# Two of four batches get their residual added by channels on GpSimd during the recurrence, and the run-up is 10 tokens

## The chip, the cores and the metric

The kernel runs on one core of a Trainium2 chip. Five engines work side by side, each through its own instructions in order: TensorE (PE, with its weight loads shown as PEld), VectorE (DVE), ScalarE (ACT), GpSimd (POOL) and SyncE (SP, which here issues nearly all DMAs). The metric is the device time of one execution in microseconds (us), the median of a few runs. Lower is better.

## The reference

The input is x with 4 batches, 128 channels and 64 x 64 = 4096 tokens, in float32. All arithmetic here is in float32.

```python
x = x + conv_attention(x)                 # layer 0: full softmax attention, 64 wide, 4096 x 4096
t = tokens(x)                             # (4, 4096, 128)
t = t + causal_attention(layernorm(t))    # layer 1: 128 wide
Wx = layernorm(t) @ W.T                   # then normalised over all 4 x 4096 tokens
y0 = 0
y[n] = sigmoid(Wx[n] + y[n-1] @ V.T)      # a recurrence over the 4096 tokens of each batch
t = t + y                                 # the residual; the result goes back to (4, 128, 64, 64)
```

V is orthogonal (128 x 128), and the slope of a sigmoid is at most 0.25, so the state forgets its start quickly.

## The kernel before

There are two paths. `fast_path` does everything and at its end sets a flag when one of its assumptions did not hold; only then `general_path` computes everything again, the recurrence token by token. In the profiled execution only the fast path ran.

**Layers 0 and 1** go batch by batch, and in each by 8 blocks of 512 query tokens. An item is a pair of key tiles: `scores` (L824) writes two 512-wide products into one of two PSUM buffers, ScalarE takes the exponential into `p`, `values` (L885) multiplies it with the values two items later, and VectorE adds `p` up in `dsum` (L875) for the softmax's denominator. Work beside this (finishing a block, projections for the next batch) is cut into small tasks. A task has a slot, counted in items, in which it is due; one task at most is issued in each slot (L988 to L1016). The chain for a block of layer 1 is `finish1` (L721): denominators, projection and residual (`first`), store of the result t to DRAM in the tensor `x2` by tokens (L740), layer norm (`norm`), change from tokens to channels (`second`: VectorE's transpose of 32 x 32 squares at L659 and two rounds of DMAs through DRAM), and `third`: the product with W (L769), its statistics on VectorE (L772), and the store of Wx over the block's own place in `xs` by ScalarE (L782). A scheduler then orders each engine's instructions, so that a task's instructions may stand a little before or after those of its neighbours.

**The recurrence** runs on 256 chunks of 16 tokens at once in each batch, so that a step is one 128 x 256 matmul per batch (L1077), one VectorE instruction (L1079: scale times Wx plus the product) and one ScalarE sigmoid (L1082), for four batches in turn. The start of a chunk is not known, so 11 tokens (`WARM`) of the chunk before are run first from a state of 0.5; after the 16 real steps the end of every chunk is compared with the start that the next chunk used (`gap`, L1106 to L1112), and the norm of the difference per channel over a batch's chunks must be at most `TOL` = 1e-6.

**The residual** (`residual`, L1089) of every batch comes after that. The states lie by channels, the result is stored by tokens: TensorE transposes four 128 x 128 pieces into a PSUM bank (L1096), VectorE adds them into `xr` (L1098), which holds the batch's t as loaded from `x2` (L1033), and after every second addition SyncE issues a store of 512 KB (L1100). There are 32 additions and 16 stores. The host transposes the output at the end.

Of the kernel before, what the change touches and what calls it, by code (L numbers as in the profile page):

```python
# [9 lines left out]
F32 = mybir.dt.float32  # L10
AF = mybir.ActivationFunctionType
ALU = mybir.AluOpType
# [5 lines left out]
CHUNK = 1024  # L18
LN_EPS = 1e-5
BN_EPS = 1e-5  # L20


@with_exitstack
def general_path(
# [11 lines left out]
    f_vT: bass.AP,  # L36
    f_gamma: bass.AP,
    f_beta: bass.AP,
    out: bass.AP,
):  # L40
    nc = tc.nc
    B, C, N = x.shape
# [240 lines left out]
    with tc.tile_pool(name="wx", bufs=1) as wxp, tc.tile_pool(name="fwork", bufs=3) as wk:  # L283
        wx = wxp.tile([P, N, B], F32, name="wx")
        stats = wxp.tile([P, B * NB, nc.vector.BN_STATS_DIM], F32, name="stats")
        with tc.tile_pool(name="ps_ln", bufs=2, space=PSUM) as ps_ln, tc.tile_pool(
            name="ps_wx", bufs=3, space=PSUM
        ) as ps_wx:
            for b in range(B):

                def project(blk, xhat, b=b):
                    wp = ps_wx.tile([P, BLK], F32, tag="w", name="wx_ps")
                    nc.tensor.matmul(wp, lhsT=wf, rhs=xhat, start=True, stop=True)
                    nc.vector.bn_stats(stats[:, b * NB + blk, :], wp)
# [12 lines left out]
        shift = wxp.tile([P, 1], F32, name="shift")  # L307
        nc.vector.tensor_tensor(shift, mv[:, 0:1], scale, ALU.mult)
        nc.vector.tensor_tensor(shift, beta, shift, ALU.subtract)

        STEPS = BLK // B
        with tc.tile_pool(name="ys", bufs=3) as ysp, tc.tile_pool(
            name="ps_y", bufs=2, space=PSUM
        ) as ps_y, tc.tile_pool(name="ps_o", bufs=2, space=PSUM) as ps_o:

            def preload(kb):
                wn = wk.tile([P, STEPS, B], F32, tag="wn", name="wn")
                nc.vector.tensor_scalar(wn, wx[:, ts(kb, STEPS), :], scale, shift, ALU.mult, ALU.add)
                ps = ps_y.tile([P, STEPS, B], F32, tag="y", name="y_ps")
                nc.tensor.matmul(ps, lhsT=ident, rhs=wn, start=True, stop=False, skip_group_check=True)  # L320
                return ps

            nblk = N // STEPS
            prev = None
            nxt = preload(0)
            for kb in range(nblk):
                ps = nxt
                y = ysp.tile([P, STEPS, B], F32, tag="y", name="y")
                for t in range(STEPS):
                    if prev is not None:  # L330
                        nc.tensor.matmul(
                            ps[:, t, :], lhsT=vf, rhs=prev, start=False, stop=t == STEPS - 1, skip_group_check=True
                        )
                    nc.scalar.activation(y[:, t, :], ps[:, t, :], AF.Sigmoid)
                    prev = y[:, t, :]
                    if t == STEPS // 2 and kb + 1 < nblk:
                        nxt = preload(kb + 1)
                o = ysp.tile([P, B, STEPS], F32, tag="o", name="o")
                nc.gpsimd.tensor_tensor(o, xs[:, :, ts(kb, STEPS)], y.rearrange("p t b -> p b t"), ALU.add)
                op = ps_o.tile([P, B, P], F32, tag="o", name="oT_ps")  # L340
                for b in range(B):
                    nc.tensor.transpose(op[:, b, :], o[:, b, :], ident)
                oT = ysp.tile([P, B, P], F32, tag="oT", name="oT")
                nc.vector.tensor_copy(oT, op)
                nc.sync.dma_start(out=out[:, ts(kb, STEPS), :].rearrange("b n c -> n b c"), in_=oT)

# [3 lines left out]
def fast_path(  # L350
# [12 lines left out]
    f_vT: bass.AP,  # L363
    f_gamma: bass.AP,
    f_beta: bass.AP,
    out: bass.AP,
    flag: bass.AP,
):

# [8 lines left out]
    TPB = BLK // P  # L378
    SHIFT = 32.0
    LOW, HIGH = 1e-25, 1e25  # L380
    WARM, TOL, STEPS = 11, 1e-6, 16
    NCH = N // STEPS
    CPB = BLK // STEPS
    S = nc.vector.STREAM_SQUARE_SIZE
# [8 lines left out]

    xs = xpool.tile([P, B, N], F32, name="xs")

    x2 = dram.tile([B, N, P], F32, name="x2")

    def load(engine, name, shape, *parts):
        t = const.tile(shape, F32, name=name)
# [70 lines left out]
    with tc.tile_pool(name="batch", bufs=1) as batch, tc.tile_pool(name="rows", bufs=2) as rowp, tc.tile_pool(  # L470
# [250 lines left out]
        def finish1(b, g):  # L721
# [10 lines left out]
            def first():  # L732
                if final:

                    nc.scalar.activation(spare, agg[:, 0:1], AF.Sigmoid)
                denominators(1, b, g, mem["own"])
                joined(1, b, g, projected(1, agg))
                if final:
                    warm(9, agg[:, : BLK // 2])
                nc.sync.dma_start(  # L740
                    out=x2[b, ts(g, BLK)].rearrange("(j p) c -> p j c", p=P),
                    in_=xs[:, b, ts(g, BLK)].rearrange("p (j c) -> p j c", c=P),
                )
                mem["xh"] = wk.tile([P, TPB, P], F32, tag="xh2", name="xh2")
                mem["of"] = moments(b, g)

# [3 lines left out]
            def second():  # L750
# [9 lines left out]
                for q in range(Q):  # L760
# [2 lines left out]
                        in_=sq[ts(q, S)].rearrange("r c j t -> r c (j t)"),  # L763
                    )
                nc.sync.dma_start(out=mem["xhT"], in_=by_c.rearrange("c r q k -> (c r) (q k)"))

            def third():
                wp = misc("wx_ps")
# [28 lines left out]
            if not final:  # L797
                yield 1, norm
            yield 2, second
            yield 1 if final else 6 if g < 2 or g == NB - 1 else 4, third  # L800


# [219 lines left out]


    with tc.tile_pool(name="xr", bufs=1) as xrp, tc.tile_pool(name="y", bufs=2) as yp, tc.tile_pool(
        name="ps_y", bufs=1, space=PSUM
    ) as ps_y, tc.tile_pool(name="ps_r", bufs=4, space=PSUM) as ps_r:

        HALVES = NCH // P
        by_chunk = lambda t: t.rearrange("b (h q s) c -> b h q s c", q=P, s=STEPS)
        xr = xrp.tile([P, B, HALVES, STEPS, P], F32, name="xr")  # L1030
        for b in range(B):
            for h in range(HALVES):
                nc.sync.dma_start(out=xr[:, b, h], in_=by_chunk(x2)[b, h])  # L1033

        mv = xrp.tile([P, nc.vector.BN_AGGR_DIM], F32, name="mv")
        nc.vector.bn_aggr(mv, ends)
# [17 lines left out]

        assert HALVES * TPB == NB
        early = xrp.tile([P, B, TPB, NCH], F32, name="early")
        late = xs.rearrange("p b (r h k q) -> p b k r h q", h=HALVES, r=TPB, q=P)

        def states(b, s):
            return pair(early[:, b, s]) if s < TPB else late[:, b, s // TPB - 1, s % TPB]

        def step(b, s):

            wx = by_step[:, b, s % STEPS]
            if s == -1:
                y = start[:, b, 1:]
            elif s < 0:
                y = yp.tile([P, NCH], F32, tag=f"y{b}", name="y")  # L1070
            else:
                y = states(b, s)
            if prev[b] is None:
                nc.scalar.activation(grid(y), wx, AF.Sigmoid, scale=scale, bias=shift_half)
            else:
                ps = ps_y.tile([P, NCH], F32, tag=f"y{b}", name="y_ps")
                nc.tensor.matmul(ps if s < 1 else pair(ps), lhsT=vf, rhs=prev[b], start=True, stop=True)  # L1077
                z = yp.tile([P, NCH], F32, tag=f"z{b}", name="z")
                nc.vector.scalar_tensor_tensor(  # L1079
                    grid(z), in0=wx, scalar=scale, in1=grid(ps), op0=ALU.mult, op1=ALU.add  # L1080
                )
                nc.scalar.activation(y, z if s < 0 else pair(z), AF.Sigmoid, bias=shift)  # L1082
            prev[b] = start[:, b, :NCH] if s == -1 else y

        for s in range(-WARM, STEPS):
            for b in range(B):
                step(b, s)

        def residual(b):  # L1089

            for h in range(HALVES):
                for s0 in range(0, STEPS, TPB):
                    part = slice(s0 - TPB, s0 + TPB)
                    ps = ps_r.tile([P, TPB, P], F32, tag="r", name="yT_ps")
                    for j in range(TPB):
                        nc.tensor.transpose(ps[:, j], states(b, s0 + j)[:, h], ident)  # L1096
                    t = xr[:, b, h, ds(s0, TPB)]
                    nc.vector.tensor_tensor(t, t, ps, ALU.add)  # L1098
                    if s0 % (2 * TPB):
                        nc.sync.dma_start(out=by_chunk(out)[b, h, :, part], in_=xr[:, b, h, part])  # L1100

        for b in range(B - 1):
            residual(b)


        gap = xrp.tile([P, B], F32, name="gap")  # L1106
        for b in range(B):
            ps = ps_y.tile([P, NCH], F32, tag=f"y{b}", name="gap_ps")
            nc.tensor.matmul(pair(ps), lhsT=ident, rhs=prev[b], start=True, stop=False)
# [72 lines left out]
```

## Time and profile before

| | us |
|---|---|
| median of 3 runs | 2064.52 (2064.33 to 2066.47) |
| the profiled execution: its time | 2065.22 |
| its span in the profile | 2063.5 |
| last attention instruction (end of the layers) | about 1971 |
| recurrence: first sigmoid to last VectorE step | 1987.21 to 2036.6 |
| 32 residual additions on VectorE | 2036.5 to 2055.9 |
| 16 output stores issued | 2037.8 to 2055.95 |
| span's end | 2063.5 |

The page lists the busy time of each engine, the chain of work that ended last, and the costliest groups. Where times of single instructions are given, they are counted from the start of the span. A line of the windows view gives, for one stretch, the busy time of each engine with its number of instructions, the clock that TensorE was granted (1.00 is full), the mean busy share of the 16 DMA engines and what they moved.

### The profile page before, as it was taken

The page shows a single profiled execution, that of the slowest core. Times are in us where ns is not written, and L with a number is a line of the kernel's source. Part 1 is how long each engine was busy: PE and PEld are TensorE (multiplying, and loading weights), DVE is VectorE, ACT ScalarE, POOL GpSimd, SP SyncE. Part 2 cuts the span into 40 slices and gives each one's busy share as a digit, 9 for nine tenths or more (in the row PEclk, how much of TensorE's full clock was granted, in tenths as well). Part 3 has the DMA queues.
Part 4 walks back from the last instruction along what each step waited for, and adds up shares of the span by engine and source line. Part 5 has one row for each costly group of instructions (what it writes and reads, how often), then busy time and mean ns, then how long its engine had stood idle before and what let it go on. Part 6 is the DMA issues. An engine that isn't in the chain of part 4 may idle for free.

```text
span 2063.5 us, 30798 instructions
## 1 busy us (share of the span) xinstructions
PE 2046.0 (99%) x11716; PEld 896.4 (43%) x11716; DVE 1492.2 (72%) x2865; ACT 990.1 (48%) x1071; POOL 135.5 (7%) x221
## 2 busy tenths in 40 slices
PE   9999999999999999999999999999999999999998
PEld 3333354444333345444333335544433334544456
DVE  4899867455889986644679987754588998764578
ACT  5666633323666643333466663332366664333365
POOL 1000011000000001000000001100000001100000
PEclk9999999999999999999999999999999999999999
DMA  4111012220100111231011101222000111110044
GB/s 113 43 23 23 12 42 51 69 67 16 57 8 17 23 28 46 62 77 41 17 43 22 23 12 42 47 67 72 16 17 5 19 23 28 41 43 25 16 169 165
DMA packets 207148, 89.03 MB, mean 43 GB/s; under 512 B 140960, under 2 KB 189600, under 8 KB 205968
## 3 DMA queue, kind: packets, MB, share of 16 engines
q1 hardware_dynamic: 205984, 86.42, 16.4%
q8 instruction: 94, 1.54, 0.3%
q14 instruction: 62, 0.51, 0.1%
q0 software_dynamic: 288, 0.39, 0.1%
q10 hardware_dynamic: 720, 0.16, 0.0%
HBM read 45.84 MB, written 36.89 MB: 40 GB/s over the span
## 4 chain that ended last, share of the span: by engine, by line
PE 97%; DVE 1%; issue 1%; DMA 0%; ACT 0%; POOL 0%; DVEq 0%; POOLq 0%; ACTq 0%
PE s_ps L844 22%; PE acc L903 22%; PE s_ps L835 22%; PE acc L895 21%; PE o_ps L614 3%; PE y_ps L1077 2%; PE r_ps L577 1%; PE wx_ps L769 1%; PE kr_ps L520 1%; PE v_ps L532 1%; DVE xr L1098 1%; PE warm_ps L484 0%; DMA swap<-kr 0%; ACT p L849 0%; DMA out_x<-xr 0%
## 5 line engine op out<-in xcount | busy, mean ns | idle before, releaser
L875 DVE TENSOR_TENSOR dsum<-dsum,p 128x1024 f32<-128x1024 f32 x676 | 826.0, 1222 | 430.2 <-ACT p L851 312.3
L849 ACT ACTIVATE p<-s_ps,nshift 128x1024 f32<-128x1024 f32 x512 | 569.6, 1117 | 315.0 <-PE s_ps L835 304.4
L851 ACT ACTIVATE p<-s_ps 128x1024 f32<-128x1024 f32 (+2 forms) x288 | 274.5, 953 | 605.5 <-PE s_ps L844 603.2
L895 PE MATMUL acc<-p,v 64*64 64x512 f32 x4096 | 529.2, 590 | 0.0
L835 PE MATMUL s_ps<-swap,kr 64*64 64x512 f32 x2048 | 524.1, 591 | 2.5 <-ACT p L849 1.6
L835 PE MATMUL s_ps<-kr 64*64 64x512 f32 x2048 | 524.1, 591 | 0.0
L844 PE MATMUL s_ps<-rows,xhT 128*128 128x512 f32 (+3 forms) x1152 | 502.9, 559 | 0.0
L903 PE MATMUL acc<-p,xh 128*128 128x512 f32 (+3 forms) x1152 | 500.8, 557 | 0.0
L903 PEld LDWEIGHTS acc<-p,xh 128*128 128x128 f32 x1152 | 216.2, 190 | 244.3 <-issue 233.5
L844 PEld LDWEIGHTS s_ps<-rows,xhT 128*128 128x128 f32 x1152 | 213.8, 190 | 242.4 <-issue 204.6
L895 PEld LDWEIGHTS acc<-p,v 64*64 64x64 f32 x4096 | 155.5, 133 | 281.7 <-issue 269.8
L835 PEld LDWEIGHTS s_ps<-swap,kr 64*64 64x64 f32 x2048 | 139.6, 133 | 141.1 <-issue 125.2
L835 PEld LDWEIGHTS s_ps<-kr 64*64 64x64 f32 x2048 | 139.7, 133 | 138.0 <-issue 133.8
L638 POOL TENSOR_TENSOR ln_rstd<-ln_var,mhalf 128x4 f32<-128x4 f32 x64 | 89.4, 1397 | 1102.1 <-DVE ln_var L636 1102.1
L883 DVE TENSOR_TENSOR dsum<-dsum,p 128x256 f32<-128x256 f32 (+1 forms) x120 | 54.9, 493 | 66.8 <-POOL p L855 66.8
L624 DVE SCALAR_TENSOR_TENSOR xs<-o_ps,recs,xs 128x128 f32<-128x128 f32 x256 | 75.0, 341 | 3.8 <-PE o_ps L614 0.5
L645 DVE TENSOR_SCALAR xh<-xs,ln_mv,ln_rstd 128x128 f32<-128x128 f32 x256 | 71.4, 342 | 2.2
L855 POOL TENSOR_SCALAR_AFFINE_SELECT p<-p 128x128 f32<-128x128 f32 x128 | 35.4, 300 | 466.6 <-ACT p L851 451.8
L633 DVE BATCH_NORM_STATS2 ln_st<-xs 128x6 f32<-128x128 f32 x256 | 63.3, 270 | 0.0
L782 ACT COPY xs<-wx_ps 128x512 f32<-128x512 f32 x31 | 18.1, 585 | 74.6 <-DVE stats L772 68.4
L873 DVE COPY dsum<-p 128x1024 f32<-128x1024 f32 x60 | 41.0, 684 | 12.1 <-ACT p L851 7.8
L1079 DVE SCALAR_TENSOR_TENSOR z<-xs,scale,y_ps 128x256 f32<-128x256 f32 x104 | 46.8, 480 | 2.9 <-PE y_ps L1077 1.7
(138 smaller groups left out, 984.6 us busy)
## 6 DMA issues: line engine op xcount, KB each, us to landing
xs<-in_xT SPq DMA_DIRECT2D x32, 256.0 KB, 2.9
by_r<-sqT SPq DMA_DIRECT2D x128, 64.0 KB, 2.2
xhT<-by_r SPq DMA_DIRECT2D x128, 64.0 KB, 2.0
x<-xs SPq DMA_DIRECT2D x32, 256.0 KB, 2.3
xr<-x SPq DMA_DIRECT2D x8, 1024.0 KB, 12.6
out_x<-xr SPq DMA_DIRECT2D x16, 512.0 KB, 4.7
by_c<-sqT SPq DMA_DIRECT2D x124, 64.0 KB, 1.8
xhT<-by_c SPq DMA_DIRECT2D x31, 256.0 KB, 2.6
```

What stands on the lines that cost most here:

```text
L614: nc.tensor.matmul(op[:, ts(j, P)], lhsT=agg[:, ts(j, P)], rhs=wv1 if layer else wo2, start=True, stop=True)
L624: nc.vector.scalar_tensor_tensor(t, in0=op[:, ts(j, P)], scalar=rec[:, j : j + 1], in1=t, op0=ALU.mult, op1=ALU.add)
L633: nc.vector.bn_stats(st[:, j], xs[:, b, ds(g * BLK + j * P, P)])
L638: nc.gpsimd.tensor_tensor(y, var, mhalf, ALU.pow)
L645: nc.vector.tensor_scalar(dst[:, j], xs[:, b, ds(g * BLK + j * P, P)], mv[:, j, 0:1], y[:, j : j + 1], ALU.subtract, ALU.mult)
L835: nc.tensor.matmul(ps[c * M : c * M + M, off : off + n], lhsT=bs[it.b].kr[part, h, ds(t % (NT // 2) * P + c * M, M)], rhs=rows[h], start=True,
L844: nc.tensor.matmul(ps[:, off : off + n], lhsT=lhsT, rhs=rhs, start=True, stop=True)
L849: nc.scalar.activation(it.p[:, :off], ps[:, :off], AF.Exp, bias=nshift)
L851: nc.scalar.activation(it.p[:, :off], ps[:, :off], AF.Exp, scale=float(P) ** -0.5)
L875: nc.vector.tensor_tensor(flat, flat, it.p, ALU.add)
L895: nc.tensor.matmul(bt.acc[h * M : h * M + M, r], lhsT=bt.v[part, t % (NT // 2), t // (NT // 2)], rhs=it.p[part, o : o + n], start=it.first ...
L903: nc.tensor.matmul(bt.acc[:, 0, q0:], lhsT=bt.xh[:, t], rhs=it.p[:, o : o + n], start=it.first and h == 0, stop=it.last and h == 1,)
```

## The change

- The run-up becomes 10 tokens (`WARM` = 10) and the tolerance 2e-6.
- Batches 0 and 1 (`BY_C` = 2) keep their t by channels too: in `finish1` the store of t by tokens goes away for them, and a new task `kept`, one slot after `second`, transposes the block's 32 x 32 squares on VectorE (as L659 does) and stores them to `x2c` in four DMAs of 64 KB, in pieces of 128 bytes. `third` follows `kept`.
- Before the recurrence `x2c` is loaded into `xc` by 8 DMAs of 512 KB into 32 partitions each; `xr` has two batches in place of four, so 4 loads of 1 MB in place of 8.
- After each of the 16 real steps GpSimd adds the states of batches 0 and 1 to `xc` (one 128 x 512 addition, in which `xc` is read with a step of 16 elements), and SyncE stores the sum: 256 KB, in pieces of 1 KB.
- States of batches 0 and 1 lie in 8 groups of 32 elements in place of 2 of 128.
- `residual` is left for batches 2 and 3. The output buffer holds two batches in one order and two in the other; the host puts both right.
- `general_path` changes in the same way; it is not shown.

```diff
-    WARM, TOL, STEPS = 11, 1e-6, 16
+    WARM, TOL = 10, 2e-6
-    x2 = dram.tile([B, N, P], F32, name="x2")
+    x2c = dram.tile([BY_C, NB, S, Q, BLK], F32, name="x2c")
+    x2t = dram.tile([B - BY_C, N, P], F32, name="x2t")
...
-                nc.sync.dma_start(
-                    out=x2[b, ts(g, BLK)].rearrange("(j p) c -> p j c", p=P),
-                    in_=xs[:, b, ts(g, BLK)].rearrange("p (j c) -> p j c", c=P),
-                )
+                if b >= BY_C:
+                    nc.sync.dma_start(
+                        out=x2t[b - BY_C, ts(g, BLK)].rearrange("(j p) c -> p j c", p=P),
+                        in_=xs[:, b, ts(g, BLK)].rearrange("p (j c) -> p j c", c=P),
+                    )
...
+            def kept():
+                sq = squares(xs[:, b, ts(g, BLK)].rearrange("p (j c) -> p j c", c=P))
+                to = x2c[b, g].rearrange("r c (j q t) -> r c j q t", q=Q, t=S)
+                for q in range(Q):
+                    nc.sync.dma_start(
+                        out=to[:, :, :, q].rearrange("r c j t -> r (c j) t"),
+                        in_=sq[ts(q, S)].rearrange("r c j t -> r (c j) t"),
+                    )
...
             yield 2, second
+            if b < BY_C:
+                yield 1, kept
             yield 1 if final else 6 if g < 2 or g == NB - 1 else 4, third
...
+        xc = xrp.tile([P, BY_C, NCH, STEPS], F32, name="xc")
+        for b in range(BY_C):
+            for c in range(Q):
+                nc.sync.dma_start(
+                    out=xc[ts(c, S), b].rearrange("r (g k) s -> r g (k s)", g=NB),
+                    in_=x2c[b, :, :, c].rearrange("g r n -> r g n"),
+                )
...
+        def add(s):
+            t = sums.tile([P, BY_C, NCH], F32, tag="sum", name="sum")
+            by_grid = lambda t: t.rearrange("p b (g c) -> p b g c", c=CPB)
+            ins = nc.gpsimd.tensor_tensor(by_grid(t), by_step[:, :BY_C, s], by_grid(xc[:, :, :, s]), ALU.add)
+            tc.keep_in_program_order(ins)
+            tc.keep_in_program_order(nc.sync.dma_start(out=out_c[:, :, s].rearrange("b c k -> c b k"), in_=t))
+
         for s in range(-WARM, STEPS):
             for b in range(B):
                 step(b, s)
+            if s >= 0:
+                add(s)
...
-        for b in range(B - 1):
+        for b in range(BY_C, B - 1):
             residual(b)
```

More of the change, by code (lines that the diff above doesn't have):

```diff
@@ L20 @@
 BN_EPS = 1e-5
+STEPS = 16
+BY_C = 2
 @with_exitstack
@@ L38, in general_path @@
     f_beta: bass.AP,
-    out: bass.AP,
+    out_c: bass.AP,
+    out_t: bass.AP,
 ):
@@ L339, in general_path @@
                 nc.gpsimd.tensor_tensor(o, xs[:, :, ts(kb, STEPS)], y.rearrange("p t b -> p b t"), ALU.add)
[L340 to L343, printed above, removed]
+                S = out_c.shape[2]
+                K = STEPS // S
+                for b in range(BY_C):
+                    oc = ysp.tile([P, S, K], F32, tag="oc", name="oc")
+                    nc.vector.tensor_copy(oc, o[:, b].rearrange("p (k s) -> p s k", s=S))
+                    nc.sync.dma_start(out=out_c[b, :, :, ts(kb, K)], in_=oc)
+                op = ps_o.tile([P, B - BY_C, P], F32, tag="o", name="oT_ps")
+                for b in range(BY_C, B):
+                    nc.tensor.transpose(op[:, b - BY_C, :], o[:, b, :], ident)
+                oT = ysp.tile([P, B - BY_C, P], F32, tag="oT", name="oT")
                 nc.vector.tensor_copy(oT, op)
-                nc.sync.dma_start(out=out[:, ts(kb, STEPS), :].rearrange("b n c -> n b c"), in_=oT)
+                nc.sync.dma_start(out=out_t[:, ts(kb, STEPS), :].rearrange("b n c -> n b c"), in_=oT)
 @with_exitstack
@@ L365, in fast_path @@
     f_beta: bass.AP,
-    out: bass.AP,
+    out_c: bass.AP,
+    out_t: bass.AP,
     flag: bass.AP,
@@ L1024, in fast_path @@
     with tc.tile_pool(name="xr", bufs=1) as xrp, tc.tile_pool(name="y", bufs=2) as yp, tc.tile_pool(
+        name="sums", bufs=3
+    ) as sums, tc.tile_pool(
         name="ps_y", bufs=1, space=PSUM
     ) as ps_y, tc.tile_pool(name="ps_r", bufs=4, space=PSUM) as ps_r:
+        xc = xrp.tile([P, BY_C, NCH, STEPS], F32, name="xc")
+        for b in range(BY_C):
+            for c in range(Q):
[3 more added lines that the diff above has]
+                )
         HALVES = NCH // P
         by_chunk = lambda t: t.rearrange("b (h q s) c -> b h q s c", q=P, s=STEPS)
-        xr = xrp.tile([P, B, HALVES, STEPS, P], F32, name="xr")
-        for b in range(B):
+        xr = xrp.tile([P, B - BY_C, HALVES, STEPS, P], F32, name="xr")
+        for b in range(B - BY_C):
             for h in range(HALVES):
-                nc.sync.dma_start(out=xr[:, b, h], in_=by_chunk(x2)[b, h])
+                nc.sync.dma_start(out=xr[:, b, h], in_=by_chunk(x2t)[b, h])
         mv = xrp.tile([P, nc.vector.BN_AGGR_DIM], F32, name="mv")
@@ L1057, in fast_path @@
         assert HALVES * TPB == NB
-        early = xrp.tile([P, B, TPB, NCH], F32, name="early")
+        early = xrp.tile([P, B - BY_C, TPB, NCH], F32, name="early")
         late = xs.rearrange("p b (r h k q) -> p b k r h q", h=HALVES, r=TPB, q=P)
         def states(b, s):
-            return pair(early[:, b, s]) if s < TPB else late[:, b, s // TPB - 1, s % TPB]
+            if b < BY_C:
+                return by_step[:, b, s]
+            return pair(early[:, b - BY_C, s]) if s < TPB else late[:, b, s // TPB - 1, s % TPB]
         def step(b, s):
             wx = by_step[:, b, s % STEPS]
+            shaped = (lambda t: t) if s < 0 else grid if b < BY_C else pair
             if s == -1:
@@ L1076, in step @@
                 ps = ps_y.tile([P, NCH], F32, tag=f"y{b}", name="y_ps")
-                nc.tensor.matmul(ps if s < 1 else pair(ps), lhsT=vf, rhs=prev[b], start=True, stop=True)
+                nc.tensor.matmul(ps if s < 1 else shaped(ps), lhsT=vf, rhs=prev[b], start=True, stop=True)
                 z = yp.tile([P, NCH], F32, tag=f"z{b}", name="z")
@@ L1081, in step @@
                 )
[L1082 removed]
+                nc.scalar.activation(y, shaped(z), AF.Sigmoid, bias=shift)
             prev[b] = start[:, b, :NCH] if s == -1 else y
+        def add(s):
[4 more added lines that the diff above has]
+            tc.keep_in_program_order(nc.sync.dma_start(out=out_c[:, :, s].rearrange("b c k -> c b k"), in_=t))
         for s in range(-WARM, STEPS):
@@ L1096, in residual @@
                         nc.tensor.transpose(ps[:, j], states(b, s0 + j)[:, h], ident)
-                    t = xr[:, b, h, ds(s0, TPB)]
+                    t = xr[:, b - BY_C, h, ds(s0, TPB)]
                     nc.vector.tensor_tensor(t, t, ps, ALU.add)
                     if s0 % (2 * TPB):
-                        nc.sync.dma_start(out=by_chunk(out)[b, h, :, part], in_=xr[:, b, h, part])
-        for b in range(B - 1):
+                        tc.keep_in_program_order(
+                            nc.sync.dma_start(out=by_chunk(out_t)[b - BY_C, h, :, part], in_=xr[:, b - BY_C, h, part])
+                        )
+        for b in range(BY_C, B - 1):
             residual(b)
@@ L1108, in fast_path @@
             ps = ps_y.tile([P, NCH], F32, tag=f"y{b}", name="gap_ps")
-            nc.tensor.matmul(pair(ps), lhsT=ident, rhs=prev[b], start=True, stop=False)
+            nc.tensor.matmul((grid if b < BY_C else pair)(ps), lhsT=ident, rhs=prev[b], start=True, stop=False)
             nc.tensor.matmul(ps, lhsT=minus, rhs=start[:, b, 1:], start=False, stop=True)
@@ L1168 @@
     }
-    y = nc.dram_tensor("out_x", (b, h * w, c), F32, kind="ExternalOutput").ap()
+    y = nc.dram_tensor("out_x", (b, c * h * w), F32, kind="ExternalOutput").ap()
+    k = h * w // STEPS
+    y = [y[:BY_C].rearrange("b (c s k) -> b c s k", s=STEPS, k=k), y[BY_C:].rearrange("b (n c) -> b n c", c=c)]
     layer0 = [ins[n] for n in ("in_x", "in_c_wqT", "in_c_wkT", "in_c_wvT", "in_c_woT")]
@@ L1174 @@
             flag = fp.tile([1, 1], mybir.dt.int32, name="flag")
-            fast_path(tc, layer0[0], ins["in_xT"], *layer0[1:], *[ins[n] for n in ("in_a_wqT", "in_a_wkT", "in_a_wv")], *ffn, y, flag)
+            fast_path(tc, layer0[0], ins["in_xT"], *layer0[1:], *[ins[n] for n in ("in_a_wqT", "in_a_wkT", "in_a_wv")], *ffn, *y, flag)
             bad = nc.values_load(flag[0:1, 0:1])
             with tc.If(bad > 0):
-                general_path(tc, *layer0, *[ins[n] for n in ("in_a_wq", "in_a_wk", "in_a_wv")], *ffn, y)
+                general_path(tc, *layer0, *[ins[n] for n in ("in_a_wq", "in_a_wk", "in_a_wv")], *ffn, *y)
     r = run_bass_kernel_spmd(nc, [arrays], core_ids=[0])
     y = np.asarray(r.results[0]["out_x"])
-    return np.ascontiguousarray(y.transpose(0, 2, 1)).reshape(b, c, h, w)
+    y_c = y[:BY_C].reshape(-1, c, STEPS, k).transpose(0, 1, 3, 2).reshape(-1, c, h, w)
+    y_t = y[BY_C:].reshape(-1, h * w, c).transpose(0, 2, 1).reshape(-1, c, h, w)
+    return np.concatenate([y_c, y_t])
```

## The prediction

> **What bounds the kernel now.** I read the page first. TensorE is busy all the time, and the chain that ended last runs through it:
>
> ```profile
> PE 2046.0 (99%) x11716; PEld 896.4 (43%) x11716; DVE 1492.2 (72%) x2865; ACT 990.1 (48%) x1071; POOL 135.5 (7%) x221
> PE 97%; DVE 1%; issue 1%; DMA 0%; ACT 0%; POOL 0%; DVEq 0%; POOLq 0%; ACTq 0%
> xr<-x SPq DMA_DIRECT2D x8, 1024.0 KB, 12.6
> out_x<-xr SPq DMA_DIRECT2D x16, 512.0 KB, 4.7
> ```
>
> The share is an average, so I cut the end, where the change lies, into stretches:
>
> ```profile
> 1996.00:2004.00 8.00, 8.00 (x37) 5.21 (x36) 7.96 (x18) 8.00 (x19) 0.00 (x0) 1.00 1.01 424
> 2012.00:2020.00 8.00, 8.00 (x38) 5.74 (x37) 7.72 (x19) 7.89 (x19) 0.00 (x0) 1.00 0.00 0
> 2040.00:2044.00 4.00, 4.00 (x34) 3.69 (x32) 4.00 (x8) 0.48 (x2) 0.00 (x0) 1.00 1.00 402
> 2056.00:2060.00 4.00, 0.00 (x0) 0.00 (x0) 0.00 (x0) 0.00 (x0) 0.00 (x0) 0.84 0.92 353
> ```
>
> The columns after the length are PE, PEld, DVE, ACT, POOL, the clock, the DMA share and GB/s. From 2004 to 2036 GpSimd is idle, and the DMAs nearly so. From 2038 to 2060 the DMAs are full at about 402 GB/s and VectorE is full too. The chain of waits gives the recurrence's beat, the instructions' own answers the store's:
>
> ```profile
> 1988.01 20.68 PE y_ps L1077 x90
> L1098 DVE TENSOR_TENSOR xr<-xr,yT_ps x32: 664/680/682, 2036.5 to 2055.3; 128x512 f32<-128x512 f32 x32
> L1100 SPq DMA_DIRECT2D out_x<-xr x16: 332/332/1278, 2037.8 to 2055.9; - x16
> DMA to landing us min/median/max: 2.6/4.7/5.8
> ```
>
> A product of the recurrence stands twice in the records, so 90 are 45 products in 20.68 us: 0.455 us each, 1.81 to 1.82 us a step of four batches, back to back on TensorE. The stores are issued every (2055.95 - 2037.82)/15 = 1.21 us; the first lands after 2.6 us, the late ones after up to 5.8, because the DMAs are full.
>
> **The change, part by part.**
>
> *One run-up token less.* Four products go: -1.81 us. VectorE's last step then ends at 2034.8 in place of 2036.6. Other bounds of the step do not enter: VectorE and ScalarE keep the same beat.
>
> *16 additions and 8 stores less at the end.* The first store goes out 1.22 us after the last step, at 2036.0, the eighth 7 x 1.21 = 8.5 us later, at 2044.5; now the sixteenth goes out at 2055.95. So eight beats go: -9.7 us. The landing of the last one grew from 2.6 to 5.8 us over 15 stores; at the eighth it is 2.6 + 3.2 x 7/15 = 4.1 us: -1.7. But the last sum (256 KB, 0.65 us at 402 GB/s) is stored just ahead: +0.65. Together -10.7; what follows the last landing (the closing semaphores, 1.7 us) stays. What is late next: the last landing comes at about 2049; TensorE's closing branch (5.4 us after its last transpose) would end near it.
>
> *The new additions on GpSimd.* States of batches 0 and 1 are ready for step 0 at 1988.72 + 37 x 0.455 + 0.48 + 0.51 = 2006.5, for step 15 at 2034.4. No addition of this size is in the trace. A selection on 128 x 128 takes 0.294 us and a memset of 128 x 4 takes 0.102, so 128 elements stream in 0.19 us. One input: 0.10 + 4 x 0.19 = 0.87 us, the lower end. Twice four whole selections, 2.35 us, is the upper end (two inputs, one of them read in steps of 64 bytes). I take two inputs at the streaming rate, 0.10 + 8 x 0.19 = 1.6 us, the only row that reads and writes at length being the selection. That is under a step of 1.85 us (1.81 and the transposes between), so the last ends at 2036.0, just when the first residual store is ready: 0. All 16 sum stores stand ahead of the residual stores in SP's queue, so above 1.85 us the queue waits for the sixteenth: at 2.35 it ends at 2006.5 + 16 x 2.35 = 2044.1, and the end moves by 8 us. Nothing else waits for GpSimd: its next instruction is the reading of the flag.
>
> [...]
>
> *Do the additions disturb VectorE?* This is the wait I looked for longest:
>
> ```profile
> 117.27 2.55 DVE L875 TENSOR_TENSOR dsum<-dsum,p 128x1024 f32<-128x1024 f32 x2
> 117.44 1.92 POOL L638 TENSOR_TENSOR ln_rstd<-ln_var,mhalf 128x4 f32<-128x4 f32 x1 [0.77 <-DVE ln_var L636]
> ...
> 315.91 0.87 DVE L624 SCALAR_TENSOR_TENSOR xs<-o_ps,recs,xs 128x128 f32<-128x128 f32 x3
> 316.31 0.54 POOL L855 TENSOR_SCALAR_AFFINE_SELECT p<-p 128x128 f32<-128x128 f32 x2 [2.29 <-issue]
> ```
>
> Beside VectorE's sums of two SBUF tensors GpSimd's power took 1.92 us in place of its 1.01. Beside the form that takes one operand from PSUM neither was stretched (three in 0.87 us, two selections in 0.54). The recurrence's L1079 is of that second form: 0; the other end is a whole addition per step, a rival below.
>
> *Loads.* `xc` takes the place of `kr`, `swap` and values, so its first load needs only the last attention product (about 1971) and the others follow the last store of t at 1977.0, where the eight `xr` loads now start at 1983.8. 8.4 MB at 424 GB/s are 20 us: all there by 2000, wanted at 2006.5 and 2034.8. 0; hidden by the run-up (18 us), and without it a late `xc` would delay the additions one for one. ScalarE's last copy of Wx waits for that store of t, which lands in 2.3 us and stands ahead of seven of the loads: 5 us to spare.
>
> [...]
>
> *States in 8 groups of 32.* ScalarE's read of such groups (L1074) took 0.59 against 0.51 us: 32 x 0.08 = 2.6 us is one end, 0 the other. I take 0: the scattered copy L782 (0.586) costs what the plain ones do (0.58), and TensorE sets the beat.
>
> *In the layers.* Per block of batches 0 and 1 there are 3 more DMAs on SP and one more VectorE transpose (0.71 us), and `third` comes a slot later. TensorE shows no gap inside layer 1, so 14 of the 16 cost nothing. The last block's lie in the next batch's layer 0, whose slot is 1.72 us, and there it is tight already:
>
> ```profile
> 529.83 0.71 DVE L659 STREAM_TRANSPOSE sqT<-xh 128x512 f32<-128x512 f32 x1
> 530.46 10.49 DVE L875 TENSOR_TENSOR dsum<-dsum,p 128x1024 f32<-128x1024 f32 x8
> 540.87 0.69 DVE L772 BATCH_NORM_STATS2 stats<-wx_ps 128x6 f32<-128x512 f32 x1
> ...
> 541.59 0.59 ACT L782 COPY xs<-wx_ps 128x512 f32<-128x512 f32 x1 [3.16 <-DVE stats L772]
> 542.08 2.13 ACT L849 ACTIVATE p<-s_ps,nshift 128x1024 f32<-128x1024 f32 x2
> ...
> 543.25 0.65 PE L835 MATMUL s_ps<-swap,kr 64*64 64x512 f32 x2 [0.49 <-ACT p L849]
> ```
>
> ScalarE's copy waits for VectorE's statistics, which stand behind eight sums; the exponentials stand behind the copy, and TensorE waits 0.49 us. In the changed program a transpose (0.71), a ninth sum (1.33) and the denominators' sum (0.72) come ahead of the statistics, and the copy comes one exponential later. The next exponential moves from 542.08 to 544.84 and ends at 545.95; the product that waits for it was due at 544.48: a wait of 1.5 us, 1.0 more. Two such boundaries (batch 1 and 2 begin): +2.1 us; ends 0 and 4.
>
> *Sum:* -1.8 - 10.7 + 2.1 = -10.4 us. The profiled execution took 2065.22 (span 2063.5 and 1.7 around it), so it would be 2054.8; the median shown is 0.7 lower: 2054.1 us.
>
> **Rivals.**
>
> 1. *GpSimd becomes the bound.* An addition of 1.9 to 2.45 us: at 2.35 the time is 2062. For it: the upper end of the bounds; against: the selection's rate.
> 2. *Slower: the additions hold VectorE.* If L1079 has to wait while an addition of 1.6 us reads, each of the 16 real steps grows by up to 1.6: +25.6, 2080. It decides from 0.65 us a step (10.4/16). For it: GpSimd and VectorE do hold each other at 117.44; against: 316.31. An addition above 2.5 us would do the same.
> 3. *The slot costs more in the layers*, at several blocks rather than two: +4 to +8, so 2058 to 2062. Against: no gap in layer 1 now.
> 4. *No cost at the boundaries and the full landing gain:* 2051 to 2052.
> 5. *The flag goes up.* With 10 tokens the ends must meet within 2e-6; the recurrence on these inputs in float32 leaves 1.1e-6 (0.67e-6 with 11, against 1e-6). Raised, the general path would add 4096 steps of at least 0.38 + 0.51 us: over 3600 us.
>
> **How the numbers follow.** Forecast 55%, rival 4 12%, rival 1 14%, rival 3 9%, rival 2 9%, flag 1%. The forecast's own range is 2052 to 2057. The low end is 2051.3 (landing without the last sum's 0.65, boundaries free); the high end 2061.5 takes in most of rivals 1 and 3 and leaves out rival 2 and the flag. 0.2% (4.1 us) is about what a measurement can tell from no change; faster than 2060.4 are the forecast, rival 4 and half of rivals 1 and 3: 0.85; within 0.2%: 0.05; slower: 0.10.
>
> **What would show it.** 100 VectorE steps and 16 additions in place of 104 and 32; eight residual stores 1.21 us apart from about 2036; 16 GpSimd additions near 1.6 us, 1.85 apart, beside VectorE steps still of 0.48 us; loads done by 2000; waits of about 1.5 us in place of 0.49 near 546 and 1037 and 0.6 unchanged near 1526; a span of about 2053. I am wrong if the additions exceed 1.85 us, if VectorE's steps grow beside them, or if TensorE shows gaps in layer 1.

## The result, and the profile after

The changed kernel takes 2057.88 us (median of 7 runs, 2056.80 to 2059.62), the kernel before 2064.8 us (7 runs). The ratio is 0.9964, interval 0.9955 to 0.9973: 5.6 to 9.3 us less. The forecast was 2054.1 us. The profiled execution took 2056.91 us with a span of 2055.2 us; before it was 2065.22 and 2063.5. So the profiles differ by 8.3 us where the prediction's sum was 10.4.

Four marks in the trace cut this difference up: TensorE's resumption after its first long wait, its first den_ps product of the final block, its first product of the recurrence, and the end of VectorE's last step there.

| stretch | before | after | difference | predicted |
|---|---|---|---|---|
| start to TensorE's resumption (13.90; 13.58) | 13.90 | 13.58 | -0.32 | 0 |
| the layers, to the den_ps product (1974.07; 1976.00) | 1960.17 | 1962.42 | +2.25 | +2.1 |
| final block, to the first product of the recurrence (1988.01; 1989.94) | 13.94 | 13.94 | 0 | 0 |
| recurrence, to the end of VectorE's last step (2036.60; 2036.66) | 48.59 | 46.72 | -1.87 | -1.81 |
| from there to the last landing (2061.74; 2052.76) | 25.14 | 16.10 | -9.04 | -10.7 |
| from the last landing to the end | 1.78 | 2.45 | +0.67 | 0 |

The first row is chance: over the profiles of this case that have such a wait TensorE resumed between 13.15 and 14.26.

The instructions' own answers for the changed kernel, GpSimd's additions, their stores, the residual stores and VectorE's steps of the recurrence:

```profile
L1129 POOL TENSOR_TENSOR sum<-xs,xc x16: 1521/1530/1549, 2008.6 to 2036.5; 128x512 f32<-128x512 f32 x16
  ACT xs L1122: 23.5, 8
L1131 SPq DMA_DIRECT2D out_x<-sum x16: 372/372/389, 2010.1 to 2038.0; - x16
DMA to landing us min/median/max: 2.1/2.1/3.1
L1151 SPq DMA_DIRECT2D out_x<-xr x8: 332/332/418, 2038.5 to 2048.1; - x8
DMA to landing us min/median/max: 2.7/3.8/4.7
L1119 DVE SCALAR_TENSOR_TENSOR z<-xs,scale,y_ps x100: 479/481/482, 1990.7 to 2036.2; 128x256 f32<-128x256 f32 x100
```

An addition takes 1.53 us (1.6 was taken). The first starts at 2008.6 and the sixteenth at 2036.5, 1.86 us apart on average, so GpSimd pauses 0.3 us in each step and keeps up with the recurrence. VectorE's steps stay at 0.48 us beside them, with a spread of 3 ns. The end, cut as before (the columns are those of the prediction):

```profile
2040.00:2044.00 4.00, 3.83 (x27) 3.30 (x25) 2.47 (x7) 1.43 (x6) 0.00 (x0) 1.00 1.02 406
2044.00:2048.00 4.00, 2.37 (x21) 2.08 (x21) 4.00 (x8) 0.00 (x0) 0.00 (x0) 1.00 0.91 356
2048.00:2052.00 4.00, 0.00 (x0) 0.00 (x0) 0.04 (x1) 0.00 (x0) 0.00 (x0) 0.81 0.72 273
```

VectorE, full there in the kernel before, now has a pause; the timeline says where:

```profile
2040.17 1.28 DVE L1148 TENSOR_TENSOR xr<-xr,yT_ps 128x512 f32<-128x512 f32 x2
...
2042.97 0.17 DVE L1166 TENSOR_SCALAR count<-gap 128x4 f32<-128x4 f32 x1 [1.53 <-ACT sq L1164]
2043.05 0.69 DVE L1148 TENSOR_TENSOR xr<-xr,yT_ps 128x512 f32<-128x512 f32 x1
```

The comparison of the ends stands behind three batches' additions (24) in the kernel before, and behind one batch's (8) now. It waits 1.53 us for ScalarE's fourth sum of squares, which waits for TensorE's eight `gap_ps` products (16 records). Between two stores pass 2.96 us in place of 1.2 (issued at 2041.47 and 2044.43). The prediction had no such step.

And the boundary of batch 1, where the prediction put 1.0 us:

```profile
542.66 0.69 DVE L949 TENSOR_TENSOR den<-dsum 128x512 f32<-128x512 f32 x1
...
543.27 0.69 DVE L796 BATCH_NORM_STATS2 stats<-wx_ps 128x6 f32<-128x512 f32 x1
...
544.00 0.59 ACT L806 COPY xs<-wx_ps 128x512 f32<-128x512 f32 x1 [4.10 <-DVE stats L796]
...
545.65 0.65 PE L861 MATMUL s_ps<-swap,kr 64*64 64x512 f32 x2 [1.43 <-ACT p L875]
```

TensorE waits 1.43 us (1.5 was predicted), at batch 2's boundary 1.42, at batch 3's 0.48.

### The profile page after: what moved, and what is told of

Its sections match the earlier page's. It is cut to its first block, busy times and chain, and to the rows that moved or that the text cites. A ratio compares the mean times of both kernels' runs of the same rounds, so it can differ in the third digit from the quotient of the medians.

```text
span 2055.2 us, 30785 instructions
## 1 busy us (share of the span) xinstructions
PE 2035.8 (99%) x11644; PEld 890.5 (43%) x11644; DVE 1487.8 (72%) x2861; ACT 988.2 (48%) x1067; POOL 154.0 (7%) x237
## 5 line engine op out<-in xcount | busy, mean ns | idle before, releaser
L1119 DVE SCALAR_TENSOR_TENSOR z<-xs,scale,y_ps 128x256 f32<-128x256 f32 x100 | 45.0, 481 | 2.8 <-PE y_ps L1117 1.7
```

## The experiments

Spans below are those of profiled executions; they differ by chance in the start (up to 1.1 us), so stages are compared from mark to mark.

**The run-up alone.** The kernel before, with

```diff
-    WARM, TOL, STEPS = 11, 1e-6, 16
+    WARM, TOL, STEPS = 10, 2e-6, 16
```

> The kernel before with 10 run-up tokens and a tolerance of 2e-6, nothing else changed. Theory: the recurrence starts and runs as before and has four products less, 4 x 0.453 = 1.81 us; everything behind it comes 1.81 us earlier: span 2061.7 in place of 2063.5. Rival: something that the run-up hid (the loads of t, about 20 us long, or the parameters) comes due and takes part of it back: span between 2062 and 2063.5.

Measured: span 2061.0, ratio to the kernel before 0.9988 (0.9979 to 0.9997), median 2063.65. From the first product to the end of VectorE's last step pass 46.78 us in place of 48.59: 1.81 less, as expected; 0.7 of the span is the start (13.19 in place of 13.90). The loads are still in time.

**Is VectorE's pause worth anything?** Two kernels move it. The first places the comparison four additions later (and holds the additions in that order):

```diff
+        residual(B - 1, [0])
         count = xrp.tile([P, B + 2], F32, name="count")
 ...
-        residual(B - 1)
+        residual(B - 1, [1])
```

> The changed kernel with the comparison of the ends (count, total, flag on VectorE) placed four residual additions later. In the changed kernel VectorE stands still from 2041.45 to 2042.97. Theory A (VectorE's place for the comparison is the cause: it waits for ScalarE's fourth sum of squares, and the additions behind it with it): the pause goes, the last store is issued 1.5 us earlier, span 2053.7. Theory B (TensorE is the cause: its 16 products of the comparison, 3.46 us, stand ahead of the transposes of the last batch): the ninth addition still waits for transposes that end at about 2042.65, only 0.4 us go, span about 2054.8.

The second also takes the products away from TensorE:

```diff
-            nc.tensor.matmul((grid if b < BY_C else pair)(ps), lhsT=ident, rhs=prev[b], start=True, stop=False)
-            nc.tensor.matmul(ps, lhsT=minus, rhs=start[:, b, 1:], start=False, stop=True)
+            nc.gpsimd.tensor_tensor(shape(diff), prev[b], shape(start[:, b, 1:]), ALU.subtract)
```

> As the run with the later comparison, and the differences of the ends are formed on GpSimd (four subtractions of 128x256) in place of TensorE's 16 products. Theory A: no change against the later comparison alone. Theory B: VectorE's 16 residual additions run without a pause, 16 x 0.6 = 9.6 us from 2036.6, the last store is issued at about 2046.3 in place of 2048.07, and the span is about 2053.5. Rival C (the stores are held by the DMAs, 8 x 1.3 us at 402 GB/s, whatever VectorE does): the last landing moves by under 0.5 us, span 2054.7 or more.

Measured: spans 2056.0 and 2054.7, medians 2057.87 and 2057.49. The timelines of VectorE, first of the later comparison alone:

```profile
2040.05 1.27 DVE L1148 TENSOR_TENSOR xr<-xr,yT_ps 128x512 f32<-128x512 f32 x2
2042.73 2.48 DVE L1148 TENSOR_TENSOR xr<-xr,yT_ps 128x512 f32<-128x512 f32 x4 [1.40 <-PE yT_ps L1146]
```

and of the one with GpSimd's differences:

```profile
2036.11 7.25 DVE L1148 TENSOR_TENSOR xr<-xr,yT_ps 128x512 f32<-128x512 f32 x12
...
2037.51 2.61 POOL L1163 TENSOR_TENSOR diff<-xs,start 128x256 f32<-128x256 f32 x4
```

So of the pause itself theory B is right: with the comparison out of the way VectorE waits 1.40 us for transposes that stand behind TensorE's products, and without those products 12 additions follow each other (0.95 us are then lost later, around the flag). But the time does not follow (theory B had put the spans at 2054.8 and 2053.5): from VectorE's last step to the last landing pass 16.10 us in the changed kernel, 17.03 with the later comparison (its flag now interrupts the last additions), and 16.03 without the products. Rival C's number holds (whether its reason, full DMAs, does is asked next): without the products the last store goes out 0.8 us earlier (10.60 us after VectorE's last step in place of 11.41), but needs 5.4 us to land in place of 4.7, and 0.1 us is left.

**What the stores wait for.** The landings of the eight residual stores, from the trace's semaphore events (us):

```
changed kernel     2041.52 2042.85 2044.16 2045.40 2047.10 2049.34 2051.51 2052.76
without products   2041.03 2042.37 2043.66 2044.93 2046.24 2047.77 2051.02 2052.22
```

Up to the fourth they come 1.3 us apart (512 KB at about 402 GB/s), then there are steps of 2.2 and 3.2 us. In the same stretch instructions are fetched, by packets of 8 and 16 KB in the DMA engines' own list: 0.87 us at 2046.7 and 1.16 us at 2048.2 in the changed kernel. To tell whether these make the steps, a kernel leaves out the reading of the flag, the branch on it and the general path behind it:

```diff
-            bad = nc.values_load(flag[0:1, 0:1])
-            with tc.If(bad > 0):
-                general_path(tc, *layer0, ...)
```

> The changed kernel without the reading of the flag, the branch on it and the general path behind it (the recomputation for inputs that miss the assumptions is left out; on these inputs it doesn't run). In the changed kernel instruction fetches of 8 and 16 KB (0.87 and 1.16 us each) come at 2046.7 and 2048.2 while stores are in flight, the landings of the sixth and seventh store step by 2.24 and 2.17 us in place of 1.25, and 2.4 us pass from the last landing to the end. Theory (jumping over the general path brings these fetches, and they delay one of the DMA engines that the stores use): the landings keep a step of about 1.25 to 1.3 us, the last comes at about 2051 in place of 2052.76, and less than 2 us follow; span about 2053. Rival 1 (the landings are late because the DMAs are full, fetches or not): the last landing stays at about 2052.5, span 2054.5 or more. Rival 2 (the fetches come in order of the program, branch or not): the steps of 2.2 us stay.

Measured: span 2052.3, median 2055.13, ratio to the kernel before 0.9952 (0.9936 to 0.9969). The DMA answers for 2046 to 2050, first of the changed kernel:

```profile
q1 hardware_dynamic: 415, 1.52, 96.6%
q14 instruction: 3, 0.02, 2.3%
q8 instruction: 1, 0.02, 1.8%
...
out_x<-xr SPq DMA_DIRECT2D x3, 512.0 KB, 4.6
```

and of the one without the branch:

```profile
q1 hardware_dynamic: 443, 1.62, 99.6%
...
out_x<-xr SPq DMA_DIRECT2D x3, 512.0 KB, 2.8
```

```
without the branch 2041.68 2042.97 2044.27 2045.55 2047.27 2048.50 2049.85 2051.08
```

In the changed kernel nine packets of instructions are fetched from 2046.7 to the end; in the kernel without the branch none is after 2031.1. Without fetches the stores after the pause land every 1.2 to 1.35 us, 2.8 us after their issue in place of 4.6; from VectorE's last step to the last landing pass 14.28 us in place of 16.10, and then 1.21 in place of 2.45 to the end. The branch, with what hangs on it, costs 3.1 us in the changed kernel (1.82 and 1.24). The last landing (2051.08) and the time after it come where the theory put them, so it is the fetches that make the landings late. Which of the things left out calls for the fetches, this run does not separate. VectorE's pause is still there (2041.61 to 2044.58 between two stores), and the landings around it are 1.72 us apart: that the pause would cost something once the fetches are gone is argued, not tried.

In the changed kernel's trace ScalarE and GpSimd branch on the flag at 2045.03 and 2045.05, TensorE's branch runs from 2046.58 to 2050.84, and the first of the nine fetches is at 2046.74. Not every fetch beside which a landing is late follows a branch on the flag, though: in the kernel before, that of 2050.29 comes ahead of the first such branch (2053.15). The DMA answers add that from 2046 to 2050 the fetches take 4.1% of the DMA engines' time; the stores have 96.6% beside them and 99.6% without.

**The boundaries.** The extra slot alone is taken out again:

```diff
-            yield 1 if final else 6 if g < 2 or g == NB - 1 else 4, third
+            yield 1 if final else 5 if b < BY_C and g == NB - 1 else 6 if g < 2 or g == NB - 1 else 4, third
```

> The changed kernel with the last task of block 7 of batches 0 and 1 due one slot sooner, so that VectorE's new transpose stays but the extra slot goes. Theory (predicted working: the transpose alone shifts the statistics by 0.5 to 0.7 us, the slot does the rest): TensorE's waits near 546 and 1038 fall from 1.43 to about 0.95 us, span 2054.2. Rival 1 (the transpose is absorbed by VectorE's slack, the slot is all of it): waits of 0.5, span 2053.4. Rival 2 (the transpose is all of it): waits of 1.43 stay, span 2055.2.

```profile
541.04 0.69 DVE L796 BATCH_NORM_STATS2 stats<-wx_ps 128x6 f32<-128x512 f32 x1
541.76 0.59 ACT L806 COPY xs<-wx_ps 128x512 f32<-128x512 f32 x1 [3.75 <-DVE stats L796]
...
543.41 0.65 PE L861 MATMUL s_ps<-swap,kr 64*64 64x512 f32 x2 [1.08 <-ACT p L875]
```

The waits fall to 1.08 and 1.09 us (0.95 was expected, 0.5 and 1.43 by the rivals), and the layers take 1961.37 in place of 1962.42 us: -1.05, half of what the change costs there (the two waits account for 0.68 of it). The transpose makes about 0.6 of the 0.94 us that a boundary's wait grew by, the slot the rest. (The span, 2056.8, is higher in spite of it; the final block takes 2.6 us longer at a lower clock of TensorE, see the last section. The median is 2055.87.)

If the cause is that the statistics queue behind VectorE's backlog of sums, a task that comes when the backlog is gone should wait for nothing:

```diff
-            yield 1 if final else 6 if g < 2 or g == NB - 1 else 4, third
+            yield 1 if final else 13 if g == NB - 1 else 6 if g < 2 else 4, third
```

> The changed kernel with the last task of block 7 of batches 0, 1 and 2 due 13 slots after the transpose in place of 6. Theory (the statistics stand behind VectorE's backlog of sums, and ScalarE's copy and its exponentials behind the statistics; the backlog shrinks by 0.4 us a slot): with the backlog gone, TensorE's waits near 546, 1038 and 1528 (1.43, 1.42 and 0.48 us) go to nearly nothing, and the layers end about 3.5 us earlier, span about 2051.5. Rival (whatever slot the task has, its copy holds the exponentials by the same amount): the waits move to other times and stay at 0.5 to 1.4 us, span about 2055.

> The kernel before with the last task of block 7 due 13 slots after the transpose in place of 6, nothing else changed. Theory (the waits at the three boundaries, 0.49, 0.49 and 0.62 us before, come from the same queue on VectorE and go with the slot): 1.6 us less and some tenths of smaller gaps, span about 2061.7 in place of 2063.5. With the slot moved in both, the change alone would then be worth about 10 us (2061.7 against 2052.0). Rival (the late task costs something of its own where there is no added transpose): span 2063 to 2064.

The first is this edit in the changed kernel, the second in the kernel before. The stretches around the three boundaries, of the changed kernel:

```profile
540.00:560.00 20.00, 18.57 (x166) 6.03 (x168) 16.16 (x16) 12.09 (x12) 0.19 (x1) 1.00 0.31 107
1030.00:1060.00 30.00, 28.58 (x258) 9.54 (x254) 24.18 (x25) 18.44 (x18) 0.19 (x1) 1.00 0.22 73
1520.00:1550.00 30.00, 29.52 (x270) 10.17 (x266) 24.88 (x26) 19.30 (x19) 0.00 (x0) 1.00 0.03 8
```

and with the late task:

```profile
540.00:560.00 20.00, 20.00 (x182) 6.79 (x178) 17.29 (x18) 13.10 (x14) 1.12 (x1) 1.00 0.33 107
1030.00:1060.00 30.00, 29.78 (x270) 10.19 (x266) 24.91 (x25) 19.72 (x19) 1.12 (x1) 1.00 0.22 72
1520.00:1550.00 30.00, 30.00 (x278) 10.47 (x274) 24.84 (x26) 19.63 (x20) 0.00 (x0) 1.00 0.02 2
```

TensorE's first column is full but for 0.22 us. The layers take 1958.55 us (-3.87 against the changed kernel); the span is 2052.0, the median 2053.46, the ratio to the kernel before 0.9938 (0.9925 to 0.9952). The kernel before gains 2.31 us in the layers by the same edit (1957.86; span 2060.6, median 2063.33). So with the late task in both kernels the change costs 0.69 us in the layers in place of 2.25, and is worth 9.9 us by the medians (about 10 was expected). The changed kernel with the late task, one number changed in one line, is as fast as any version found here and faster than both kernels.

**How near GpSimd is to being the bound.** A second addition per step whose result is not used:

```diff
+            spare = sums.tile([P, NCH], F32, tag="spare", name="spare_sum")
+            tc.keep_in_program_order(nc.gpsimd.tensor_tensor(grid(spare), by_step[:, 0, s], grid(xc[:, 0, :, s]), ALU.add))
```

> The changed kernel with a second GpSimd addition in every step, batch 0 alone (128x256), whose result is not used. GpSimd's work per step is then 1.53 + 0.8 = 2.35 us, over the step's 1.83. Theory of the prediction (GpSimd becomes the bound, and all residual stores wait behind the sixteenth sum in SyncE's queue): the sixteenth sum is stored at about 2046 in place of 2038.05, the eight residual stores land 8 x 1.3 us later, span about 2061. Rival 1 (VectorE is held too): VectorE's steps grow from 1.83 to 2.3 us as well. Rival 2 (the stores are late for other reasons anyway): span under 2057.

```profile
L1131 POOL TENSOR_TENSOR sum<-xs,xc x16: 1513/1523/1554, 2009.3 to 2044.0; 128x512 f32<-128x512 f32 x16
L1130 POOL TENSOR_TENSOR spare_sum<-xs,xc x16: 849/856/887, 2008.5 to 2043.2; 128x256 f32<-128x256 f32 x16
L1153 SPq DMA_DIRECT2D out_x<-xr x8: 398/1125/1560, 2046.0 to 2053.3; - x8
```

The sixteenth sum starts at 2044.0 in place of 2036.5, all residual stores wait behind it from 2046.0, and the span is 2062.3 (2061 was expected), the median 2066.29. From the first product to VectorE's last step pass 46.68 us: the recurrence is not held.

**Do the engines hold each other?** Batch 0's additions go to VectorE:

```diff
-            ins = nc.gpsimd.tensor_tensor(by_grid(t), by_step[:, :BY_C, s], by_grid(xc[:, :, :, s]), ALU.add)
-            tc.keep_in_program_order(ins)
+            for b, engine in enumerate((nc.vector, nc.gpsimd)):
+                ins = engine.tensor_tensor(grid(t[:, b]), by_step[:, b, s], grid(xc[:, b, :, s]), ALU.add)
+                tc.keep_in_program_order(ins)
```

> The changed kernel with batch 0's additions on VectorE (128x256, between the steps) and batch 1's on GpSimd, so that both engines read two SBUF operands at the same time. Theory (only VectorE's two-operand form holds GpSimd, as beside the sums of the layers): GpSimd's addition of 128x256 takes 0.8 us where it runs alone and up to 1.2 us where VectorE's addition falls into it; VectorE's step grows from 1.83 to 2.1 or 2.2 us, span about 2060. Rival 1 (no engine ever holds the other): 0.8 us in all 16. Rival 2 (VectorE has room beside TensorE): the step stays at 1.83, span 2055.

```profile
2014.70 0.85 POOL L1132 TENSOR_TENSOR sum<-xs,xc 128x256 f32<-128x256 f32 x1 [1.87 <-ACT xs L1124]
2014.78 1.24 DVE L1132 TENSOR_TENSOR sum<-xs,xc 128x256 f32<-128x256 f32 x1
2017.49 1.34 POOL L1132 TENSOR_TENSOR sum<-xs,xc 128x256 f32<-128x256 f32 x1 [1.93 <-ACT xs L1124]
2017.51 0.58 DVE L1132 TENSOR_TENSOR sum<-xs,xc 128x256 f32<-128x256 f32 x1
```

Of two additions that meet, one runs at its own length (0.85 on GpSimd, 0.58 on VectorE) and the other is stretched by most of that (1.24 and 1.34); the theory had only GpSimd stretched. The recurrence takes 51.95 us in place of 46.72, the span is 2061.3 and the median 2064.53. So the hold is real for this form. That the operand from PSUM is what spares L1119, and not its other operation, is shown by the run with GpSimd's differences: there VectorE's plain additions with one operand from PSUM (L1148) take 0.67 to 0.68 us, as in the kernel before, beside GpSimd's subtractions.

**Three batches by channels.** Both runs have BY_C = 3, the late task and the comparison behind the last additions. In the first the residual stores are on ScalarE's queue, in the second they stand in SyncE's, in turn with the last three sum stores:

```diff
-                            nc.sync.dma_start(out=by_chunk(out_t)[b - BY_C, h, :, part], in_=xr[:, b - BY_C, h, part])
+                            nc.scalar.dma_start(out=by_chunk(out_t)[b - BY_C, h, :, part], in_=xr[:, b - BY_C, h, part])
```

> Three batches added by channels on GpSimd, one as before with its stores on ScalarE's queue and the comparison of the ends behind its additions, and the late task of the first run of this group. Theory: an addition of 128x768 takes about 2.25 us, the sixteenth ends at 2008.2 + 36 = 2044.5, four residual stores go out meanwhile, the last landing is at about 2048 in place of 2052.8; the third batch's transposes cost nothing more in the layers. Span about 2049. Rival 1 (instruction fetches and the closing of the engines, which come after the flag, set the end): span 2052 or more. Rival 2 (the third transpose brings back a wait of about a microsecond at the third boundary): span 2050.

> Three batches by channels once more, with the late task 13 slots behind, but with all stores in SyncE's queue and the last three sum stores in turn with the four residual stores, so that no store waits for a semaphore slot of another queue. Theory (the 20 us of GpSimd's pause in the run with stores in two queues came from that alone): an addition of 128x768 takes 2.18 us, 16 follow each other, the sixteenth ends 54 us after the first product of the recurrence, the last store lands at about 2045, and the flag and the closing of the engines set the end: span 2049 to 2051. Rival (GpSimd is held by something else as well): the additions have pauses, span over 2055.

The first had its task 11 slots behind, not 13. Its span is 2074.1 (2049 was expected), the median 2073.25, the ratio 1.0037 (1.0024 to 1.0051), 0.4% slower than the kernel before: SyncE's fifth sum store waited until 2044.55 for a semaphore of the eight that all stores take in turn, while ScalarE's residual stores, the first issued at 2041.82, had taken some of them before it; GpSimd waited with it (23.2 us, in two waits). In one queue the pause is gone. The last store, issued at 2042.79, lands at 2049.9, 7.1 us later, with an instruction fetch of 1.69 us at 2046.8 in between; what makes up the rest was not tried. Span 2052.1 (2049 to 2051 was expected), median 2053.65, ratio 0.9943 (0.9929 to 0.9956). That is no better than two batches with the late task.

## Why the prediction was right, and where it was off

- *GpSimd's additions* (1.6 us, under the step): 1.53. *No hold on VectorE*: 0.479 to 0.482 us in all 100 steps. Both rivals needed another length or another form of instruction, and the runs with those gave them: 2.38 us of additions a step moved the end by 7 us, where the prediction had 8 for 2.35, and the split additions lengthened the recurrence from 46.72 to 51.95 us. The general path ran in none of the runs, so its 0.38 + 0.51 us a step stays the author's estimate.
- *Run-up* -1.81: -1.87, and -1.81 alone. (The beat that the prediction reads from 45 products in 20.68 us is 0.460 us each by division, not 0.455; -1.81 alone makes it 0.453.) *Boundaries* +2.1: +2.25; the waits were 1.43 and 1.42 where 1.5 was worked out. The task that comes late shows the named queue (copy behind statistics behind sums) to be the cause.
- *States in groups of 32*: 0, as taken; the recurrence takes 46.72 us with them and 46.78 with the run-up alone, and TensorE is busy for all of each stretch of 8 us from 1992 to 2032 (8.00). *Loads*: needed in time and there in time, but not at the rate assumed. The last `xc` load lands at 2000.5, the last `xr` load at 2011.1, where all was to be there by 2000: during `xc` (1984 to 1992) the DMAs, full (a share of 1.06), move 206 GB/s in place of 424. These loads go to 32 partitions each, and their packets are smaller too (2 KB, 0.17 us each, in place of 8 KB, 0.31 us); no run separates the two.
- *16 additions and 8 stores less*, -10.7: the term that was off, with -9.04 and +0.67. From VectorE's last step to the last landing the prediction's numbers make 9.7 + 4.1 + 0.65 = 14.45 us; it took 16.10. The failed step is the landing: "at the eighth it is 2.6 + 3.2 x 7/15 = 4.1 us". The growth from 2.6 to 5.8 was put down to full DMAs and scaled with the number of stores. In the kernel before it is no straight line: it comes in three jumps, from 2.86 to 3.94, from 4.05 to 5.32 and from 5.27 to 5.83 us, each beside an instruction fetch (8 KB at 2044.2; 16 KB at 2050.3 and 2058.1). With the run-up alone the 16 KB fetch comes later against the stores, 15.0 us after VectorE's last step in place of 13.7, and the jump is at the tenth store in place of the ninth. So the jumps follow the fetches, not the number of stores; in the changed kernel the sixth and seventh store bear them.
- The eighth store's landing alone does not show this: 4.69 us is close to the predicted 4.1 + 0.65, and the eighth store went out 11.41 us after the last step in place of 9.7, as if the pause were the whole error. The runs say otherwise. Without the pause the store went out at 10.60 and landed after 5.43 us, so the stretch stayed at 16.03; without the branch it went out at 11.42, pause included, and landed after 2.86 us, which makes 14.28. That this is so near the prediction's 14.45 is luck: 1.7 us more to the issue, 1.9 us less to land.
- *"What follows the last landing (the closing semaphores, 1.7 us) stays"*: it became 2.45, and 1.21 without the branch. SyncE asks for the eight semaphores in a fixed order; the last store's was the seventh before and is the third now, so five more are asked for behind it (2052.78 to 2053.50, one step of 0.39 us among them) in place of one.
- A step that was missing: the comparison of the ends loses its cover (16 of 24 additions), and VectorE waits 1.53 us. The pause is real, but taking it away gained 0.1 us: the landings beside the fetches were late in any case (5.43 us after the last issue in place of 4.69). (VectorE was not full to 2060 in the kernel before, as the prediction reads its stretches, but to 2056: its own line for 2056 to 2060 has 0.00.)

So the range held the time and the direction was right, while the forecast's own range of 2052 to 2057 was missed by 0.9 us. Of the 3.8 us between the forecast and the median, 2.1 are those of the span. The other 1.7 are no term of the sum: the forecast put the median 0.7 us below the profiled execution, and it lies 0.97 above. Three of the seven executions took 2059.25 to 2059.62 us at a mean granted clock of 0.997 or 0.998, the other four 2056.80 to 2057.88 at 0.998 or 0.999. That these three ran at half the clock for a while, as in the last section (a profile with a mean of 0.997), is a guess: they have no profile.

## What to carry to other kernels

When the end of a kernel is cut short, look at what belongs to the end (flags, branches, instruction fetches, closing semaphores): here it moved along and fell on fewer transfers, with landings 2.24 and 2.17 us apart at the sixth and seventh of eight stores in place of 1.3, and five closing semaphores behind the last landing in place of one. A growth along a row of stores is to be split into what the number does and what the end does before it is scaled. A pause of an engine is worth its length only if nothing behind it is late already; here the landing of the stores was, and taking away a pause of 1.53 us gained 0.1. A small task that stalls its queue may only stand at a bad time: look where the engine's backlog is gone before making the task cheaper (a later slot alone took 3.87 us off the layers here).

## What the runs showed of the hardware that had not been expected

VectorE was held for 2.38 us on an instruction that took 0.17 us in the changed kernel. In the run of three batches in one queue:

```profile
2036.02 6.51 POOL L1129 TENSOR_TENSOR sum<-xs,xc 128x768 f32<-128x768 f32 x3
...
2040.18 2.38 DVE L1179 TENSOR_SCALAR count<-gap 128x4 f32<-128x4 f32 x1
```

The same comparison of four columns took 0.17 us where GpSimd was idle; here it starts 0.17 us before one GpSimd addition follows another (at 2040.35) and ends just after this second one, 2.18 us long. It reads and writes SBUF alone. The run with the second addition per step has the same: there the comparison starts at 2043.30, takes 2.23 us and ends just after GpSimd's last addition (2043.98, 1.53 us long). What the two engines share, these rows do not show.

TensorE's clock fell to half in the final block, where TensorE has gaps, in the run without the extra slot:

```profile
1984.00:1988.00 4.00, 2.59 (x6) 1.21 (x5) 1.94 (x9) 0.59 (x1) 0.55 (x1) 0.50 1.06 201
1988.00:1992.00 4.00, 3.90 (x13) 2.98 (x12) 0.38 (x3) 2.08 (x4) 0.00 (x0) 0.72 1.07 202
```

The clock is 0.50 in place of 1.00, the first filling product after the gap takes 0.80 us in place of 0.48, and the recurrence begins 16.54 us after the den_ps product in place of 13.94. That is 2.6 us of this profile's span, more than the edit under test is worth. The changed kernel's profile has the same gaps there (1.02, 0.35 and 1.41 us) and keeps 1.00, so the gaps alone do not decide it. What decides in which executions it falls was not tried.
